# Layer 1 of a four-layer graph network: token transposes moved ahead of the softmax rows, layer-norm statistics moved behind both residual additions, bank order of queries and values swapped, and a copy moved ahead of the scatters at the layer's end

## The chip, the cores and the metric

The kernel runs on one core of a Trainium2 chip. The metric is the device time of one execution in microseconds (us). A core has five engines that run side by side, each with its own instruction stream: PE (matrix multiplications; its weight loads are listed as PEld), DVE (vector), ACT (activation functions and copies), POOL (a further vector engine, which here also issues the scatters) and SP (which issues most DMA transfers). [...]

## What is computed

The input `x` has 128 graphs of 64 nodes with 256 features, that is 8192 tokens; `adj` is a 64x64 adjacency shared by all graphs. Four layers follow each other, each of the form "layer norm of x plus f(x)":

```python
x = _layernorm(x + _L0_gnn_ref(x, adj, ...))   # dense attention over the 64 nodes
x = _layernorm(x + _L1_gnn_ref(x, ...))        # attention over 512 listed edges, 4 heads
x = _layernorm(x + _L2_gnn_ref(x, adj, ...))   # adj product, two matmuls, two batch norms
x = _layernorm(x + _L3_gnn_ref(x, adj, ...))   # two adj products, four LSTMs over windows
```

The change is in layer 1:

```python
Xq = (H @ W_lin.T).reshape(bt, n, h, dh)
Xv = (H @ W_val.T).reshape(bt, n, h, dh)
e = einsum('behd,hd->beh', leaky_relu(Xq[:, src] + Xq[:, dst], 0.2), a)
e = e + log(A0[src, dst] + EPS)
m = segment_max(e, src);  ex = exp(e - m[src]);  attn = ex / segment_sum(ex, src)[src]
Y = segment_sum(attn[..., None] * Xv[:, dst], src)
return Y.reshape(bt, n, d) @ W_out.T
```

## The kernel before

**Tiles.** The tokens are cut into 16 tiles `q` of 512 tokens (eight graphs each). Layers 0 and 1 run as one software pipeline over the 16 tiles: in step `q` the kernel does the edge work of tile `q` for layer 1, layer 0 for tiles `q + 1` and `q + 2`, the projections of layer 1 for tile `q + 1`, and the last steps of layer 1 for tiles `q - 3` and `q - 4`. Edge softmax is done for two tiles at once, a pair `S`; so a step with even `q` (from 2 on) also carries the softmax of the pair that has just been finished. Below, such a step is called a *pair step*, the other one a *plain step*.

**The steps.** `l0_e` ends layer 0 of a tile: residual, statistics and layer norm. `l1_t` transposes the 512 normalised tokens on PE (`transposed`, L227: two groups of four 128x128 transposes, each group into one bank, each copied out by ACT, L228). `l1_qv(q, c2)` projects half a tile: for each of two 128-token chunks it makes the queries (bank `pq`, L318) and the values (one bank `pv` for both chunks, L321); ACT and DVE take the queries out in turn (L328, L329, L330) and ACT copies the values (L331). `l1_graph` makes the edge sums `z` (L355), ACT takes the relu (L357); `reduce_heads` sums them with L346. `l1_softmax` and `l1_sums` do the scans on DVE (L367 to L374, then the exponential on ACT, L375, then L380 and L381, the last of which writes `dn`). `l1_weights` transposes the two softmax rows `e` and `dn` (L389, a bank each), takes a reciprocal on DVE (L395), multiplies (L397), scatters the result to DRAM with four indirect DMAs that POOL issues (L401), and SP loads it back as `ld` (L407). `v_a` has POOL copy `ld` into `am` (L414), multiplies on PE (L422, two banks) and copies with ACT (L426). `v_b` is the output projection (L436, two banks), the residual additions on DVE (L438), the statistics (L95, L96, L85, L98) and the layer norm on POOL (L86, then L100). `v_c` multiplies by the adjacency (L456). `l0_c` makes layer 0's scores: transposes L264, masks L267, L269, maximum L271, exponentials on ACT L274.

**Order.** A step lists what stands between its eight edge pieces. The list entries that matter here:

```python
[(l1_sums, S), (l0_b, q + 2)],
[(v_b, q - LAG - 1)],
[(l1_weights, S), (l1_t, q + 1), (l0_c, q + 2)],
[(sums, q), (l1_qv, q + 1, 0)],
[(v_c, q - LAG - 1), (v_a, q - LAG)],
```

A scheduler then places the instructions on each engine. `step` ties only PE's instructions to the list's order; DVE, ACT and POOL are ordered by the scheduler, from priorities and its own estimate of durations. So a change in the order of calls can also change the order on engines that it doesn't name. [...]

**Banks.** Layers 0 and 1 share three PSUM banks (5, 6 and 7 in the program) for everything called `m`: projections, transposes, `v_a`, `v_b`. A new use of a bank waits until its last reader is done. `z` has its own four banks, `e` one.

**The end of layer 1.** After step 15 the last pair's softmax and the last tiles' `v_a`, `v_b`, `v_c` remain. They are interleaved with blocks of layer 2's first matmul (`fill`; L749, eight matmuls of 512 columns each block, later the seven-product form L820). `given` keeps the order of the calls on PE, DVE, ACT and POOL, each call's instructions behind the last ones of the call before.

Of the kernel before, what the change touches and what calls it, by code (L numbers as in the profile page):

```python
# [8 lines left out]
F32 = mybir.dt.float32  # L9
# [8 lines left out]
P = 128  # L18
NB = 128
N = 64  # L20
D = 256
KD = D // P
HEADS = 4
# [3 lines left out]
NQ = 16  # L27
PQ = 4
# [13 lines left out]
def kernel(ctx: ExitStack, tc: tile.TileContext, i, out):  # L42
    nc = tc.nc
# [39 lines left out]
    def rsqrt(dst, var, n):  # L83

        nc.vector.tensor_scalar_add(dst, var, LN_EPS)  # L85
        nc.gpsimd.tensor_tensor(dst, dst, mhalf[:, :n], OP.pow)  # L86

    def layernorm(dst, src, n, engine):

        st = small.tile([P, n, 6], F32, name="ln_st", bufs=5)  # L90
        mv = small.tile([P, n, 2], F32, name="ln_mv", bufs=5)
        both = small.tile([P, 2, n], F32, name="ln_rs", bufs=5)
        rs, ng = both[:, 0, :], both[:, 1, :]
        for r in range(n):
            nc.vector.bn_stats(st[:, r, :], src[:, r, :])  # L95
            nc.vector.bn_aggr(mv[:, r, :], st[:, r, :])  # L96
        rsqrt(rs, mv[:, :, 1], n)
        nc.vector.tensor_scalar_mul(ng, mv[:, :, 0], -1.0)  # L98
        for r in range(n):
            engine.tensor_scalar(dst[:, r, :], src[:, r, :], ng[:, r:r + 1], rs[:, r:r + 1],  # L100
                                 op0=OP.add, op1=OP.mult)
# [8 lines left out]
    def given(do, *args, **more):  # L110
        traced = nc.cur_bb.bb.instructions
        first = len(traced)
        with ExitStack() as order:
            for e in latest.values():
                order.enter_context(tc.issue_after(e))
            r = do(*args, **more)  # L116
        for t in traced[first:]:
            if t.engine in (mybir.EngineType.PE, mybir.EngineType.DVE, mybir.EngineType.Activation,
                            mybir.EngineType.Pool):
                latest[t.engine] = t  # L120
        return r
# [8 lines left out]
    with ExitStack() as two:  # L130
# [7 lines left out]
        vp = values.enter_context(tc.tile_pool(name="vp", bufs=1, side="right"))  # L138
# [5 lines left out]
        def bank(shape, name="m", bufs=3):  # L144
            return (psm if name == "m" else ps).tile([P] + shape, F32, name=name, bufs=bufs)
# [85 lines left out]
        def token_major(q):  # L231

            return Aq(q).rearrange("p (c d) -> p c d", c=PQ)
# [70 lines left out]
        L1 = {}  # L304
# [5 lines left out]
        def l1_qv(q, c2):  # L310
            xT, v = L1[q]["xT"], L1[q]["v"]

            sp = spads[q // BPS % 2].rearrange("p (s e x b d h) -> p s e x b d h", e=2, s=2, x=2, b=BPS, d=2)
            pv = bank([2, D])
            for c in (2 * c2, 2 * c2 + 1):
                pq = bank([D + HEADS])
                for k in range(KD):
                    nc.tensor.matmul(pq, xT[:, k, c * P:(c + 1) * P], wq[:, k, :],  # L318
                                     start=k == 0, stop=k == KD - 1)
                for k in range(KD):  # L320
                    nc.tensor.matmul(pv[:, c % 2, :], xT[:, k, c * P:(c + 1) * P], wv[:, k, :],  # L321
                                     start=k == 0, stop=k == KD - 1)

                qs = work.tile([P, 2, D], F32R, name="qs", bufs=6)
                L1[q]["qs"].append(qs)
                for s in range(2):
                    r, ro = slice(s * N, (s + 1) * N), slice((1 - s) * N, (2 - s) * N)
                    nc.scalar.activation(qs[r, s, :], pq[r, :D], AF.Copy)  # L328
                    nc.vector.tensor_sub(qs[ro, s, :], pq[r, :D], qs[r, s, :].bitcast(F32))  # L329
                    nc.scalar.activation(sp[r, s, c % 2, 0, q % BPS, c // 2, :], pq[r, D:], AF.Copy, scale=SLOPE)  # L330
            nc.scalar.activation(v[:, 2 * c2:2 * c2 + 2, :], pv, AF.Copy)  # L331
# [75 lines left out]
                nc.sync.dma_start(ld[S][s * N:(s + 1) * N], half)  # L407


        def v_a(q):  # L410
            S, b = divmod(q, BPS)
            v = L1[q]["v"]
            am = vp.tile([P, PQ * HEADS, N], F32, name="am")
            nc.gpsimd.tensor_copy(am.rearrange("p (e r) n -> p e r n", e=2),  # L414
                                  ld[S].rearrange("p n (e b r) -> p b e r n", e=2, b=BPS)[:, b])
            pY = [bank([KD, PQ, N]) for _ in range(2)]
            for c in range(PQ):
                for h in range(HEADS):
                    for s in range(2):
                        r = slice(s * N, (s + 1) * N)  # L420
                        r0 = (h % 2) * 64
                        nc.tensor.matmul(pY[s][r0:r0 + 64, h // 2, c, :], v[r, c, h * 64:(h + 1) * 64],  # L422
                                         am[r, (c % 2) * 2 * HEADS + c // 2 * HEADS + h, :], start=True, stop=True)
            yT = L1[q]["yT"] = vp.tile([P, KD, PQ, 2, N], F32, name="yT")
            for s in range(2):
                nc.scalar.activation(yT[:, :, :, s, :], pY[s], AF.Copy)  # L426

        def v_b(q):
            yT = L1[q]["yT"]
            x1 = token_major(q)  # L430
            y = vp.tile([P, PQ, D], F32, name="y")
            for c2 in range(2):
                p_ = bank([2, D])
                for c in range(2):
                    for k in range(KD):
                        nc.tensor.matmul(p_[:, c, :], yT[:, k, 2 * c2 + c].rearrange("p s n -> p (s n)"),  # L436
                                         wout[:, k, :], start=k == 0, stop=k == KD - 1)
                nc.vector.tensor_add(y[:, 2 * c2:2 * c2 + 2, :], p_, x1[:, 2 * c2:2 * c2 + 2, :])  # L438
            x2 = L1[q]["x2"] = y
            layernorm(x2, y, PQ, nc.gpsimd)  # L440
            nc.sync.dma_start(x2_dram[q], x2.rearrange("p c d -> p (c d)"))

        def v_c(q, one=True):
# [125 lines left out]
        l0_d(1)  # L569
        l1_t(0)  # L570
        l1_qv(0, 0)
        l1_qv(0, 1)


# [86 lines left out]
        LAG = BPS + 1  # L661
# [4 lines left out]
        def step(do, n, *more):  # L666
            if not 0 <= n < NQ:
                return
            traced = nc.cur_bb.bb.instructions
            first = len(traced)  # L670
            if queue:
                with tc.issue_after(queue[-1]):
                    do(n, *more)
            else:
                do(n, *more)
            mine = [t for t in traced[first:] if t.engine == mybir.EngineType.PE]
            queue.extend(mine[-1:])
# [4 lines left out]
        for q in range(NQ):  # L682
            S = q // BPS - 1 if q % BPS == 0 else -1
            between = [
                [(l0_e, q + 1), (l0_a, q + 2)],
                [(sums, q if q else -1), (l1_softmax, S)],
                [(l1_sums, S), (l0_b, q + 2)],
                [(v_b, q - LAG - 1)],
                [(l1_weights, S), (l1_t, q + 1), (l0_c, q + 2)],
                [(sums, q), (l1_qv, q + 1, 0)],  # L690
                [(v_c, q - LAG - 1), (v_a, q - LAG)],
                [(l0_d, q + 2), (l1_qv, q + 1, 1)],
            ]
            for b in range(GQ):
                step(l1_graph, q, b)
                for do, n, *more in between[b]:
                    step(do, n, *more)
                if setup:
                    setup.pop(0)()
        sums(q)  # L700
        S = NQ // BPS - 1
# [55 lines left out]
        def up_block(q):  # L757
            for m in range(2):
                put(q, m, up(q, m))
                if m == 0:  # L760
                    last_tail()
            pz = [up(q, m) for m in (2, 3)]
            for m in (2, 3):
                put(q, m, pz[m - 2])
# [167 lines left out]
        def one(q):  # L932
            return lambda: up_block(q)

        def pair(q, g):
            return lambda: up_job(q, g, T[q])

        fill = [one(n) for n in range(7)] + [pair(n, g) for n in (7, 9) for g in range(2)]
        given(v_b, NQ - LAG - 1)
        fill.pop(0)()  # L940
        given(l1_sums, S)
        fill.pop(0)()
        given(v_c, NQ - LAG - 1, False)
        given(l1_weights, S)
        sums_at = {3: 7, 5: 9}
        for n, (do, q) in enumerate([(do, q) for q in range(NQ - LAG, NQ) for do in (v_a, v_b, v_c)]):
            given(do, q, *[False] * (do == v_c))
            fill[n]()
            if n in sums_at:
                T[sums_at[n]] = tile_sums(inputs(sums_at[n]))  # L950
        q = NQ - LAST - 1
# [1023 lines left out]
```

## Time and profile before

| | before |
|---|---|
| median of three timed runs | 2052.08 us (2048.62, 2052.08, 2052.64) |
| the profiled execution | 2051.53 us, of which the recorded span is 2049.7 us |
| mean granted clock of PE over the span | 0.986 of full speed |
| a pair step and a plain step together, in the middle of layers 0 and 1 | 61.25 us (the scan L372 starts at 231.12, 292.38, 353.63 us) |
| PE busy in 292 to 353 us | 58.06 of 61.00 us |
| layers 0 and 1 run until about | 523 us, their end beside layer 2 until about 616 us |

The span counts from the first to the last instruction; 1.83 us of the profiled execution lie around it. "Busy" counts an instruction from start to end; matmuls overlap, and their ends are modelled. In the answers quoted below, a line of the timeline gives start and length in us, engine, source line, operation, what it writes and reads, how many instructions are merged, and in brackets how long the engine stood idle before it and what released it. A line of the waits gives the total in us, how often, and the longest.

### The profile page before, as it was taken

To read this page: it belongs to the slowest core of one execution; us is meant where nothing else is said; L and a number is where in the kernel's file an instruction comes from. 1 tells how busy PE (TensorE), PEld (TensorE's weight loads), DVE (VectorE), ACT (ScalarE), POOL (GpSimd) and SP (SyncE) were. 2 spreads that over 40 slices of the span, in tenths; PEclk is the share of its full clock that TensorE was granted. 3 is DMA by queue.
4 is the path that set the end of the run, shared out by engine and by line. 5 is a ranking of instruction groups with operands and counts; after the bars stand their busy time and mean duration, and the time that the engine had idled before them with its cause. 6 is when DMAs were issued, how large, how long until landed. Compare 5 with 4: busy or idle time off the path is not lost.

```text
span 2049.7 us, 31505 instructions
## 1 busy us (share of the span) xinstructions
PE 1943.6 (95%) x11447; PEld 1332.9 (65%) x11447; DVE 1256.3 (61%) x2763; ACT 987.6 (48%) x1892; POOL 883.8 (43%) x1017
## 2 busy tenths in 40 slices
PE   5999999999899989899999999999999999999997
PEld 4666667766454435477677477677577667578685
DVE  7456665564457454765566865556775557764566
ACT  2766667666335633634343644343544333544333
POOL 1123334343345543564545543435443445444264
PEclk8999999999999999999999999999999999999998
DMA  5344443332112125432242243132143032131022
GB/s 134 79 65 68 79 69 54 66 50 39 37 29 60 41 103 171 158 136 98 112 143 85 77 140 139 42 126 91 52 153 120 21 113 65 44 119 78 0 65 70
DMA packets 236539, 173.84 MB, mean 85 GB/s; under 512 B 150624, under 2 KB 213600, under 8 KB 233056
## 3 DMA queue, kind: packets, MB, share of 16 engines
q1 hardware_dynamic: 234528, 169.86, 29.1%
q8 instruction: 90, 1.47, 0.3%
q0 software_dynamic: 1024, 1.05, 0.2%
q10 hardware_dynamic: 832, 0.92, 0.1%
q14 instruction: 65, 0.53, 0.1%
HBM read 110.18 MB, written 61.60 MB: 84 GB/s over the span
## 4 chain that ended last, share of the span: by engine, by line
PE 68%; DVE 17%; ACT 5%; POOL 4%; issue 4%; DMA 1%; SPq 0%; DVEq 0%; POOLq 0%; ACTq 0%
PE l L1700 25%; PE l L1656 7%; PE l L1437 4%; PE pz L820 4%; PE e L346 3%; PE m L318 2%; PE pz L749 2%; PE g L1336 2%; PE m L253 2%; PE m L321 2%; PE z L355 2%; PE pz L1017 2%; PE g L1324 2%; DVE ln_st L95 1%; DVE cell L1614 1%
## 5 line engine op out<-in xcount | busy, mean ns | idle before, releaser
L1700 PE MATMUL l<-xs,wx 128*128 128x256 f32 (+1 forms) x896 | 277.0, 400 | 5.7 <-DVE gate L1719 4.2
L1700 PE MATMUL l<-hs,wh 128*128 128x256 f32 (+1 forms) x896 | 276.5, 399 | 2.9 <-DVE hs L1564 2.1
L1715 ACT ACTIVATE kept<-l 128x256 f32<-128x256 f32 (+1 forms) x224 | 88.6, 402 | 332.2 <-PE l L1700 330.7
L86 POOL TENSOR_TENSOR ln_rs<-ln_rs,mhalf 128x2 f32<-128x2 f32 (+2 forms) x98 | 86.4, 882 | 338.1 <-DVE ln_rs L98 334.9
L1700 PE MATMUL l<-H,wx 128*128 128x256 f32 (+1 forms) x672 | 210.5, 402 | 4.3 <-DVE gate L1728 3.4
L1700 PE MATMUL l<-hid,wh 128*128 128x256 f32 (+1 forms) x672 | 208.8, 399 | 0.0
L1700 PEld LDWEIGHTS l<-xs,wx 128*128 128x128 f32 x896 | 168.6, 190 | 50.7 <-issue 5.8
L1700 PEld LDWEIGHTS l<-hs,wh 128*128 128x128 f32 x896 | 169.2, 190 | 46.8 <-DVE hs L1564 4.7
L1733 ACT ACTIVATE gate<-gate,bias 128x512 f32<-128x512 f32 (+1 forms) x280 | 170.6, 657 | 42.0 <-DVE gate L1724 34.8
L1656 PE MATMUL l<-H,wx 128*128 128x256 f32 (+5 forms) x672 | 185.2, 431 | 4.9 <-DVE H L116 2.7
L1656 PEld LDWEIGHTS l<-H,wx 128*128 128x128 f32 x672 | 118.8, 190 | 65.5 <-issue 34.2
L357 ACT ACTIVATE u<-z 128x1024 f32<-128x1024 f32 x128 | 130.3, 1025 | 63.4 <-PE z L355 62.6
L1700 PEld LDWEIGHTS l<-H,wx 128*128 128x128 f32 x672 | 125.7, 190 | 42.6 <-DVE gate L1728 7.4
L1700 PEld LDWEIGHTS l<-hid,wh 128*128 128x128 f32 x672 | 127.2, 190 | 32.0 <-issue 2.6
L1723 POOL TENSOR_TENSOR gate<-gate,kept 128x256 f32<-128x256 f32 (+1 forms) x84 | 64.9, 773 | 154.2 <-DVE kept L1721 153.9
L329 DVE TENSOR_TENSOR qs<-m,qs 64x256 fp32r<-64x256 f32 x128 | 54.1, 422 | 109.1 <-ACT qs L328 107.0
L355 PE MATMUL z<-gath_r,qs 128*128 128x512 f32 x256 | 99.9, 478 | 0.6 <-ACT u L357 0.4
L1622 ACT ACTIVATE gate<-cell 128x512 f32<-128x512 f32 (+1 forms) x88 | 58.6, 666 | 86.5 <-DVE cell L1614 64.5
L1568 POOL TENSOR_TENSOR hs<-hid 128x256 f32<-128x256 f32 (+1 forms) x28 | 27.4, 977 | 168.3 <-DVE hid L1600 85.2
L1728 DVE TENSOR_TENSOR gate<-l,gate 128x256 f32<-128x256 f32 (+1 forms) x112 | 50.0, 446 | 61.4 <-POOL gate L1723 36.4
L1610 POOL TENSOR_TENSOR cell<-gate,cell 128x512 f32<-128x512 f32 (+1 forms) x56 | 75.4, 1367 | 28.4 <-ACT gate L1733 28.4
L1717 DVE TENSOR_TENSOR gate<-l,kept 128x256 f32<-128x256 f32 (+1 forms) x112 | 49.2, 439 | 57.1 <-ACT gate L1733 32.9
(375 smaller groups left out, 4095.3 us busy)
## 6 DMA issues: line engine op xcount, KB each, us to landing
wx<-sums SPq DMA_DIRECT2D x9, 2048.0 KB
wh<-sums SPq DMA_DIRECT2D x9, 1792.0 KB
way<-st SPq DMA_DIRECT2D x54, 256.0 KB
st<-way SPq DMA_DIRECT2D x216, 64.0 KB
xin<-in_x SPq DMA_DIRECT2D x16, 512.0 KB
ld<-table SPq DMA_DIRECT2D x16, 512.0 KB
x_dram<-y SPq DMA_DIRECT2D x16, 512.0 KB
x2r<-x_dram SPq DMA_DIRECT2D x32, 256.0 KB
```

What stands on the lines that cost most here:

```text
L86: nc.gpsimd.tensor_tensor(dst, dst, mhalf[:, :n], OP.pow)
L346: nc.tensor.matmul(pes[S][n * CG:(n + 1) * CG, :], apad[:, k, CG - HEADS - r0:2 * CG - HEADS - r0], u[:, k, :], start=r0 == 0 and k == 0, ...
L355: nc.tensor.matmul(z[:, k, :], L1[q]["qs"][c][:, s, k * P:(k + 1) * P], gath_r, start=True, stop=True)
L357: nc.scalar.activation(u, z, AF.Relu)
L820: nc.tensor.matmul(self.bank[at], lhs, rhs, start=first and n == 0, stop=n == len(self.terms) - 1, skip_group_check=True)
L1437: nc.tensor.matmul(self.bank[at], lhs, rhs, start=new, stop=True, skip_group_check=True)
L1610: nc.gpsimd.tensor_tensor(c, t, c, OP.mult)
L1656: nc.tensor.matmul(b, w.raw[0][:, k, at, m, :], x, start=k == 0, stop=k == KD - 1)
L1700: nc.tensor.matmul(self.banks[j], lhs, rhs, start=src == 0, stop=src == 1)
L1715: nc.scalar.activation(self.keep(j), b, AF.Copy)
L1723: e.tensor_tensor(t[0][:, 1], t[0][:, 1], k[5], OP.add)
L1733: given(lambda: nc.scalar.activation(dst, dst, f, bias=b))
```

## The change

Five edits, in `l1_qv`, `v_a`, `v_b`, the step list and the code after the last step:

```diff
-            pv = bank([2, D])
+            pv = None
             for c in (2 * c2, 2 * c2 + 1):
                 pq = bank([D + HEADS])
+                if pv is None:
+                    pv = bank([2, D])
...
-        def v_a(q):
+        def v_m(q):
             S, b = divmod(q, BPS)
-            v = L1[q]["v"]
-            am = vp.tile([P, PQ * HEADS, N], F32, name="am")
+            am = L1[q]["am"] = vp.tile([P, PQ * HEADS, N], F32, name="am")
             nc.gpsimd.tensor_copy(am.rearrange("p (e r) n -> p e r n", e=2),
                                   ld[S].rearrange("p n (e b r) -> p b e r n", e=2, b=BPS)[:, b])
+
+        def v_a(q):
+            if "am" not in L1[q]:
+                v_m(q)
+            v, am = L1[q]["v"], L1[q]["am"]
...
-            layernorm(x2, y, PQ, nc.gpsimd)
+            with tc.issue_after(nc.cur_bb.bb.instructions[-1]):
+                layernorm(x2, y, PQ, nc.gpsimd)
...
-                [(l1_weights, S), (l1_t, q + 1), (l0_c, q + 2)],
+                [(l1_t, q + 1), (l1_weights, S), (l0_c, q + 2)],
...
+        given(l1_sums, S)
         given(v_b, NQ - LAG - 1)
         fill.pop(0)()
-        given(l1_sums, S)
+        given(v_m, NQ - LAG)
+        given(l1_weights, S)
         fill.pop(0)()
         given(v_c, NQ - LAG - 1, False)
-        given(l1_weights, S)
```

In words: the bank of the first queries is asked for before the bank of the values. The statistics of `v_b` may not be placed before its second residual addition. In each step the token transposes come before the softmax rows' transposes. At the end of layer 1, the last pair's sums come before `v_b` of tile 12, and the last pair's row transposes and scatters come one block of layer 2 earlier, with the copy `am` of tile 13 ahead of them on POOL.

The order that results on each engine, seen in the two built programs (no times are in it): the numbers of instructions and their operands are the same. On PE, in every pair step, the eight transposes L227 stand before the eight of L389, and the rest of layer 1 is in the same order; at the end, `L436, L749 x8, L389 x8, L749 x8, L456, L422` replaces `L436, L749 x16, L456, L389 x4, L749 x1, L389 x4, L749 x14, L422`. On DVE, both L438 stand before the eight statistics; in pair steps the reciprocal L395 follows behind all statistics of `v_b` (before, it stood ahead of the last of them), and the four L329 of the next projection come between L267, L269, L271 and L277. On ACT, in pair steps, the four exponentials L274 stand behind three of the four L328 (before, behind one), and the copy of the values L331 stands behind L274 and two more short instructions; in plain steps L274 stands behind one L328 (before, ahead of all). On POOL, in pair steps, the layer norm of `v_b` stands before all four scatters (before, the first scatter stood ahead of it). Waits for banks also change hands: the second row's transposes (L389, `dn`) take the bank that the first group of token transposes used, so they wait for ACT's L228 of that group; L318 of the first projection takes the bank of the `dn` row and waits for L395.

## The prediction

> **What bounds the kernel now.** I read the page's busy times and its chain first, then PE's waits over the middle of layers 0 and 1, then the timelines of one pair step, last the stretches in which PE's clock fell.
>
> ```profile
> span 2049.7 us, 31505 instructions
> PE 1943.6 (95%) x11447; PEld 1332.9 (65%) x11447; DVE 1256.3 (61%) x2763; ACT 987.6 (48%) x1892; POOL 883.8 (43%) x1017
> ...
> PE 68%; DVE 17%; ACT 5%; POOL 4%; issue 4%; DMA 1%; SPq 0%; DVEq 0%; POOLq 0%; ACTq 0%
> ```
>
> PE is the bound; no instruction goes, so only PE's idle time can. PE's waits from 170 to 540 us:
>
> ```profile
> PE m L318 <- ACT yT L426: 5.4, 10, 0.6
> PE m L227 <- ACT tT L228: 4.1, 6, 0.7
> PE m L227 <- issue: 3.3, 5, 0.7
> PE m L264 <- DVE ln_mv L96: 2.4, 5, 0.5
> PE m L389 <- DVE dn L381: 2.2, 1, 2.2
> ```
>
> Lines 2 to 5 all sit where rows and tokens are transposed in a pair step. The timeline of PE in one of them, and in the last one (q = 14):
>
> ```profile
> 301.48 0.64 PE L227 MATMUL m<-ident,A 128*128 128x128 f32 x4 [0.66 <-issue]
> 302.81 0.66 PE L227 MATMUL m<-ident,A 128*128 128x128 f32 x4 [0.69 <-ACT tT L228]
> 303.95 0.66 PE L264 MATMUL m<-ident,sb 128*128 128x128 f32 x4 [0.48 <-DVE ln_mv L96]
> 304.36 0.72 PE L355 MATMUL z<-gath_r,qs 128*128 128x512 f32 x2
> ...
> 314.89 1.15 PE L318 MATMUL m<-wq,tT 128*128 128x260 f32 x4 [0.56 <-ACT yT L426]
> ```
> ```profile
> 483.21 0.63 PE L389 MATMUL m<-ident,dn 128*128 128x128 f32 x4 [2.25 <-DVE dn L381]
> ...
> 490.78 1.15 PE L318 MATMUL m<-wq,tT 128*128 128x260 f32 x4
> ```
>
> The first wait is for the second addition (300.72 to 301.38), which stands behind half the statistics; the second for the one bank both token groups share; the third ends with the reciprocal (302.17 to 303.90), not with the L96 named. The other engines at the same place:
>
> ```profile
> 308.32 0.39 ACT L274 ACTIVATE e<-e,mx 128x128 f32<-128x128 f32 x1
> ...
> 310.71 0.58 ACT L331 ACTIVATE v<-m 128x512 f32<-128x512 f32 x1
> ```
>
> L422 needs that copy (done 311.29) and starts at 311.99: 0.7 us of slack. And the clock, by stretches:
>
> ```profile
> 122.40:129.00 6.60, 5.91 (x25) 2.92 (x28) 5.00 (x11) 2.89 (x6) 1.66 (x2) 0.50 0.76 98
> 484.00:490.60 6.60, 5.91 (x26) 2.07 (x24) 3.52 (x13) 2.22 (x3) 3.36 (x5) 0.50 0.02 5
> 554.90:557.50 2.60, 0.10 (x2) 0.01 (x2) 0.69 (x1) 0.69 (x1) 2.53 (x2) 1.00 0.05 13
> ```
>
> The seventh column is the granted clock: half speed for 6.6 us after the gaps at q = 2 (2.07 us) and q = 14 (2.25 us), at 5.91 us busy some 2.9 us lost each time; none after the gap of 2.50 us at 555, where L422 waits for POOL's copy behind four scatters.
>
> [...] L331 at 310.71 stands behind L274, and a late maximum delays the values. [...] L100 takes 4.24 us for four beside the scans (292.65), 2.16 otherwise (306.78).
>
> **The change part by part.** All from the timeline of 299 to 315 us, durations as they stand there; gains against the same instruction before.
>
> *Pair step, transposes.* PE is free at 299.79. L227's first group has its bank (copied at 297.1) and runs to 300.23; the second takes the bank of addition one (done 299.80) until 300.67; L389 of `e` that of addition two, now about 299.74 to 300.40: no wait. L389 of `dn` needs the first L228, which stands behind ACT's L357 (next instruction at 300.91), so 301.51 with its 0.60; start 301.56. L264 follows at 302.04, z at 302.45 instead of 304.36: gain 1.9.
>
> *Pair step, given back.* DVE now does all statistics first: 1.94 from 300.34 to 302.28 (as 289.51 to 291.45). Reciprocal to 303.94, one L267, four L397 (0.2 each), three L267: 305.84. L329 waits for ACT's L328, 1.18 behind L318's start (306.86, 308.04 before), now 304.95, so until 306.54; then L329, L269, L329, L271 at about 0.45 and 0.7: maximum at 308.8, before 307.4. ACT: L274 308.8 to 310.35, L330, L328, then L331 to 311.5. PE would start L422 at 304.95 + 5.13 = 310.08 and stands 1.45 for the values. ACT's next L357 starts at 311.51 (before: 312.08), L426 behind it, and L318, which waits for L426's bank, comes 0.57 earlier (314.32), no more. I take +0.57; bounds 1.9 (values not late) and -1 (maximum 1.5 later than worked out).
>
> *Plain step.* Addition two waits for PE (331.41) either way; two L95 and two L96 move behind it: the maximum comes 0.6 later (335.86 to 336.45). L274 now stands behind one L328 and ends at 338.5 instead of 337.45, but two L328 that stood behind it go with or ahead of it; L357 at 340.79 instead of 340.58, L318 0.2 later. Five pairs (q = 4 to 13): 5 x (0.57 - 0.21) = gain 1.8.
>
> *q = 2.* L227 fills the gap ahead of `dn`, its fourth row block waiting for L100 until 119.14. But `dn`'s bank waits for L228, behind two L357 (119.95 to 121.87): L389 at 122.43, 0.8 later than before (121.61). Behind the waiting L389 stand L264, z and L346, for which the layer-0 scores and ACT's relu wait; all move together. Then L264 122.92, z 123.3 instead of 125.33: gain 2.0. The gap is still 1.88, so the clock may fall again; at full clock the late maximum takes back what the clock gives, thus 2.0 either way; bounds 0.8 and 3.
>
> *q = 14.* No L95 stands between the scans: `dn` at 482.86 instead of 483.07. L389 at 482.9, z at 483.35 instead of 486.08, after a gap of 1.15: no fall of the clock. L318 waits for the reciprocal (484.97 to 486.7) and starts at 486.73 instead of 490.78: gain 4.05, of which 2.9 is the clock's. L100 now comes ahead of the scatters and is done at 490.4, L456 at 490.9.
>
> *q = 15.* Here PE waits on `v_b`'s chain: L438 (509.36), statistics, L86, L100, L414, L422 at 516.57, L426, L346 at 519.84. After the second addition stand four L95 instead of two: 1.78 to L85 instead of 1.1, loss 0.66.
>
> *The end.* Sums first: both scans at 528.2 to 530.8, additions and statistics behind, L98 at 534.5 instead of 530.6; L86 and L100 with 3.45 end at 539.1, the copy for tile 13 (1.9) at 541.0. PE: L436 to 526.1, a block of 6.95, L389 0.9, a block: L456 at 540.9, L422 at 541.95. No wait, 0.95 spare; the 2.50 go. Scatters from 541 at 2.9 each end at 550, SP's L407 starts about 553 (557.47 before), so tile 14's copy is no later. L456 of tile 13 waited 0.80 and stood stretched by 0.97 (2.07 against 1.1) for L100: L436 now stands 4 us further from it. Gain 4.3; the last tile's statistics again hold POOL, loss 0.3.
>
> *Scatters and SP.* In pair steps POOL now runs L86 and L100 first (302.3 to 305.6), then four scatters without the layer norm between them: at the 3.5 between the later ones before (309.12, 312.63, 316.19), from 305.7 to about 316.3, as late as before. So SP's L407 (318.33), the loads of x queued behind it, and the copy L414 (328.71, which ended on L407's landing) stand still: nothing. If POOL's spacing grew, L414 has 9 us until L422 at 340.52 needs it.
>
> *Bank order of queries and values.* L318 now waits for the reciprocal (303.94 against its own 304.95), so a reciprocal 1 us later would stop PE; L321 waits for L397 as before. In plain steps the first queries get the bank that is free first, as before. Nothing, with half a us either way for each pair of steps in the range.
>
> Sum: 2.0 + 1.8 + 4.05 - 0.66 + 4.3 - 0.3 = 11.2 us. After 616 us nothing differs, and PE's later waits are on DVE, ACT and POOL, so it carries to the end. The profiled execution's 2051.53 (span 2049.7, 1.83 around it) becomes 2040.3; the median lies 0.55 above that execution: **2041**.
>
> **The rivals.** *R1, everything is given back in the steps, and the clock's part is luck:* the values' wait takes the whole gain of a pair step (5 x -0.2 = -1.0), and an execution that keeps its clock gains only 0.8 at q = 2 and 1.15 at q = 14. 0.8 + 1.15 - 0.66 - 1.0 + 4.3 - 0.3 = 4.3 less than 2052.08: 2047.8. For it: three timings spread by 4 us, about the clock's price; against: the median is the higher kind. *R2, the values are not late:* if DVE runs ahead of my reckoning by 1.4, pair steps gain up to 1.9: 5 x 1.3 = 6.5 more, 2034.5. Against: the order on DVE puts L329 ahead of the maximum. *R3, slower:* the gap before L422 in each pair step grows from 1.45 to 2.1 us, a length at which the clock was seen to fall (2.07). It decides once L331 ends at 312.2, that is a maximum 0.7 later. Each of five steps then loses 0.65 and the clock's 2.9: 5 x 3.55 = 17.7 on top of 2041, about 2058.7; with the clock falling in every second one, 2051. For it: DVE's order in pair steps is the tightest of all. Against: a gap of 1.41 at 516 left the clock alone. *R4, POOL's copy is late at the end* (scans or L100 slower by 2): 2 us back, 2043, inside the range.
>
> **How the numbers follow.** A measurement tells about 0.2% here, 4.1 us. Forecast with R4 0.60, R1 0.18, R2 0.12, R3 0.10. Faster: forecast and R2 whole, R1 by a third (2048.0 is the border and R1 stands at 2047.8 with its own spread): 0.78; R1's rest and the mild form of R3 within 0.2%: 0.14; slower: R3 otherwise, 0.08. Range 2034.5 to 2048.5: R2, the forecast's own 2037 to 2045, R1.
>
> **What would show it.** In a pair step: no wait at L227, 0.3 to 0.5 at the second L389, 1.4 at L422 ending on L331, L318 about 0.6 earlier; the pair of steps at 60.9 us. No half clock near q = 14, L318 there 4 us sooner; no wait at L422 behind the scatters. Wrong if the period stays at 61.25 or grows, or if new half-clock stretches appear between 180 and 480 us.

## The result, and the profile after

The changed kernel takes 2044.78 us (median of nine runs, 2044.55 to 2046.24), the kernel before on the same chip 2050.94 (nine runs, 2048.32 to 2052.64): ratio 0.9971, 95% interval 0.9962 to 0.9980. It is 4 to 8 us faster, about half of the 11.2 us forecast, and inside the range. The profiled execution took 2044.78 us, its span is 2043.0.

The page of the changed kernel, first its busy times, then the shares of its chain:

```profile
span 2043.0 us, 31508 instructions
...
PE 1938.6 (95%) x11447; PEld 1335.4 (65%) x11447; DVE 1252.3 (61%) x2763; ACT 987.1 (48%) x1892; POOL 878.0 (43%) x1017
...
PE 69%; DVE 15%; ACT 5%; POOL 4%; issue 3%; DMA 2%; SPq 1%; DVEq 0%; POOLq 0%; ACTq 0%
```

PE has the same 11447 matmuls and is still the bound; its busy time is 5.0 us less though no instruction went: the same matmuls took less time, and a stretch at half clock is one of the things that make them longer (sixteen of `L253` took 6.34 us under it before, 3.75 at full clock after). PE's waits of the changed kernel from 170 to 540 us (total, times, longest):

```profile
PE m L428 <- ACT v L333: 7.2, 5, 1.4
PE m L320 <- ACT yT L432: 4.7, 10, 0.6
PE m L391 <- DVE y L444: 2.2, 1, 2.2
PE m L428 <- POOL am L415: 1.7, 1, 1.7
PE m L391 <- ACT tT L228: 1.5, 5, 0.3
PE e L348 <- ACT u L359: 1.2, 1, 1.2
PE z L463 <- POOL y L100: 1.0, 1, 1.0
```

(L318, L331, L389, L422, L436, L438, L456 of before are now L320, L333, L391, L428, L442, L444, L463.) The waits at L227 and L264, 9.8 us in all, are gone, and 7.2 us stand in a new place: five times 1.44 for the copy of the values. The timelines of PE and of ACT in the pair step at 300 us show both ends of it:

```profile
297.10 1.04 PE L227 MATMUL m<-ident,A 128*128 128x128 f32 x8
297.97 0.60 PE L391 MATMUL m<-ident,e 128*128 128x128 f32 x4
298.87 0.66 PE L391 MATMUL m<-ident,dn 128*128 128x128 f32 x4 [0.29 <-ACT tT L228]
...
309.12 1.16 PE L428 MATMUL m<-am,v 64*64 64x64 f32 x62 [1.44 <-ACT v L333]
...
311.76 1.14 PE L320 MATMUL m<-wq,tT 128*128 128x260 f32 x4 [0.39 <-ACT yT L432]
```
```profile
306.21 0.40 ACT L274 ACTIVATE e<-e,mx 128x128 f32<-128x128 f32 x1 [0.45 <-DVE mx L271]
...
308.46 0.60 ACT L333 ACTIVATE v<-m 128x512 f32<-128x512 f32 x1
```

ACT waits for DVE's maximum, runs the four exponentials, and only then copies the values for which PE stands. Two PE starts, of `v_c` in step after step, give the length of a pair step and a plain one together: 60.84 us (306.41 to 367.25), before 61.25 (311.00 to 372.25).

Where the time of the two profiled executions differs, stage by stage (start of the same PE instruction, after against before):

| stage | forecast gain | gain between the two profiles |
|---|---|---|
| up to 60 us, no changed instruction in it | 0 | 3.1 |
| q = 2 | 2.0 | 1.8 |
| q = 3 | 0 | -3.0 |
| q = 4 to 13 | 1.8 | 2.05 |
| q = 14 | 4.05 | 2.3 |
| q = 15 | -0.66 | -4.6 |
| the end of layer 1 | 4.3 - 0.3 | 3.7 |
| after 616 us | 0 | 1.4 |

The first and the last line are no work of the change. In the first 60 us `L253` took 6.34 us before and 3.75 after at the same place, because half clock covered it in one execution only; after 616 us PE's waits are the same within half a us each, but for one that is 1.0 us longer after, and half clock covers the last 12.6 us before and the last 9.8 after. So the changed stages gain 2.25 us between these two executions, and 4.5 us lie where the change has no part. The stages hold half clock too, 13.7 us of it before and 17.1 after between 60 and 640 us. What the change is worth on the average is therefore read from the timed runs, not from this pair.

### The profile page after: what moved, and what is told of

The parts are those of the page before. It is cut to its first block, busy times and chain, and to the rows that moved or that the text cites. A ratio compares the mean times of both kernels' runs of the same rounds, so it can differ in the third digit from the quotient of the medians.

```text
span 2043.0 us, 31508 instructions
## 1 busy us (share of the span) xinstructions
PE 1938.6 (95%) x11447; PEld 1335.4 (65%) x11447; DVE 1252.3 (61%) x2763; ACT 987.1 (48%) x1892; POOL 878.0 (43%) x1017
## 4 chain that ended last, share of the span: by engine, by line
PE 69%; DVE 15%; ACT 5%; POOL 4%; issue 3%; DMA 2%; SPq 1%; DVEq 0%; POOLq 0%; ACTq 0%
PE l L1708 25%; PE l L1664 7%; PE l L1445 4%; PE pz L827 4%; PE pz L756 3%; PE m L253 2%; PE e L348 2%; PE m L320 2%; PE m L442 2%; PE g L1344 2%; PE pz L1025 2%; PE z L357 2%; PE m L323 2%; DVE cell L1622 1%; PE g L1332 1%
## 5 line engine op out<-in xcount | busy, mean ns | idle before, releaser
L331 DVE TENSOR_TENSOR qs<-m,qs 64x256 fp32r<-64x256 f32 x128 | 53.9, 422 | 105.0 <-ACT qs L330 103.2
```

## The experiments

The kernels of one group below were timed on one chip beside the kernel before; its median there was 2050.1 (first group), 2052.7 (second), 2053.1 (third) and 2050.9 us (the last kernel). So ratios, not times, are compared between groups.

**One part alone.** Each edit was put into the kernel before; the fourth kernel is the changed one with the values' bank again asked for first.

```diff
swap_only:  [(l1_weights, S), (l1_t, q + 1), ..] -> [(l1_t, q + 1), (l1_weights, S), ..]
stats_only: + with tc.issue_after(nc.cur_bb.bb.instructions[-1]): layernorm(x2, y, ..)
end_only:   the edits of v_a, v_m and of the code after the last step
no_bank:    the changed kernel with  pv = bank([2, D])  ahead of the loop over c
```

> The kernel before, with the step list's swap alone (token transposes ahead of the softmax rows). Theory of the prediction: the swap is what takes the transposes' wait away, but with half the statistics still between the two additions the second group of L227 waits as before for addition two, so a pair of steps gets 0.2 to 0.6 us shorter (61.25 to about 60.85), q = 2 some 2 us shorter, nothing at the end: 1 to 4 us in all, about 2048. Rival, the parts need one another: the pair of steps stays at 61.25 and the time within 1 us of 2050.9. Rival, clock luck: no change in any period, only the first 60 us differ from run to run.

> The kernel before, with the statistics behind both residual additions alone. Theory of the prediction: in a plain step it costs 0.2, in a pair step it brings the rows' transposes forward by the 0.66 that the second addition waited but makes the layer-0 maximum and with it the values' copy later; q = 15 loses about 0.7. Pair of steps 60.9 to 61.4, total within 2 us of 2050.9, more likely above. Rival: it alone carries the gain of the steps (pair of steps at 60.85 or less, total 2047 or less).

> The kernel before, with the edits at the end alone (sums first, POOL's copy and the rows ahead of the scatters' wait). Theory of the prediction: 4.3 us from the wait of 2.5 at L422 and from q = 16, nothing anywhere else: 2046.6, with the pair of steps at 61.25 and the half-clock stretches near q = 2 and 14 still there. Rival: the end's gain is taken up later (PE's waits after 616 us grow), total 2050 or more.

> The changed kernel with the values' bank again taken first. Theory of the prediction: the order of the banks is worth nothing, 2044.8 within 1 us, pair of steps 60.84, the wait of some 1.4 for the values' copy still there. Rival: taking the queries' bank first is what made the wait at q = 3 grow to 2.3 or the values late; then without it the losses at q = 3 and q = 15 (3.0 and 4.6 us) go and the time is 2038 to 2041. Second rival: it carries a part of the steps' gain, then the pair of steps is above 61.

| kernel | ratio to before, 95% interval | pair and plain step |
|---|---|---|
| swap_only | 0.9997 (0.9989 to 1.0005) | 61.08 |
| stats_only | 1.0007 (0.9999 to 1.0015) | 60.98 to 61.44, on average 61.16 |
| end_only | 0.9979 (0.9969 to 0.9989) | 61.25 |
| no_bank | 0.9966 (0.9954 to 0.9979) | 60.84 |

The end alone brings 0.21%, 4.3 us, as forecast. Neither step edit brings anything alone. In the trace of swap_only, the timeline of PE shows in a pair step the wait of 0.64 that was expected there, now at the rows `e`, and at q = 15 a wait for POOL's copy that was not:

```profile
301.59 1.04 PE L227 MATMUL m<-ident,A 128*128 128x128 f32 x8
303.26 0.66 PE L389 MATMUL m<-ident,e 128*128 128x128 f32 x4 [0.64 <-DVE y L438]
...
517.80 1.98 PE L422 MATMUL m<-am,v 64*64 64x64 f32 x64 [4.96 <-POOL am L414]
```

There POOL starts the first scatter of q = 14 at 491.53, behind the layer norm of `v_b` (before: 487.10, ahead of it), and the second starts 5.56 later, so the rows come back from DRAM only at 515.8. In this profile that wait alone, 4.96 against 1.41 before, takes back some 3.5 us of what the swap gives in the other steps. In stats_only, PE's timeline of a pair step shows the waits of before moved on by one group:

```profile
302.06 0.66 PE L227 MATMUL m<-ident,A 128*128 128x128 f32 x4 [0.69 <-ACT tT L228]
303.40 0.66 PE L264 MATMUL m<-ident,sb 128*128 128x128 f32 x4 [0.69 <-ACT tT L228]
...
314.86 1.14 PE L318 MATMUL m<-wq,tT 128*128 128x260 f32 x4 [1.06 <-ACT yT L426]
```

What the additions give at the transposes is taken back at `L318`, 1.06 instead of 0.56. The bank order is worth nothing that can be told: no_bank keeps the period of 60.84 and the wait of 1.44, and the intervals of the two ratios overlap. Its rival, that the bank order made the losses at q = 3 and q = 15, is out too: the wait at q = 3 is still 2.07, and the clock still falls at q = 15.

**The steps' edits together, and the odd tiles.** Second group, with the two kernels of the next two paragraphs.

```diff
steps_only: the changed kernel without the edits at the end
stats_even: with tc.issue_after(..) only  if q % BPS == 0
```

> The changed kernel without the edits at the end: swap, statistics and bank order only. Theory that the parts add up: the swap alone (ratio 0.9997) and the statistics alone (1.0007) make nothing together, 2050.9. Theory that the two need one another (the swap only pays when the second addition no longer stands behind half the statistics): 2 to 3 us faster than before, 2047.5 to 2048.5, pair of steps at 60.84 against 61.08 (swap alone) and 61.16 (statistics alone), and the wait for the values' copy of 1.4 back in each pair step.

> The changed kernel with the statistics behind both additions only in even tiles, which the pair steps and the end's first tile take; the plain steps and q = 15 (tile 11) are as before. Theory: in q = 15 the layer norm of tile 11 is 0.66 earlier, so the two waits there (0.99 for L100's rows, 1.67 for POOL's copy) shrink by about 0.66 together, and the clock falls there less often; plain steps within 0.1 each. 0.7 to 3 us better than the changed kernel: 2042 to 2044. Rival, the odd tiles do not matter and what was lost at q = 15 was the grid of the clock's windows alone: waits of 2.6 stay, time within 1 us of 2044.8.

steps_only: ratio 0.9987 (0.9979 to 0.9995), 2.7 us; pairs of steps from 60.85 to 61.06. Alone the two step edits come to +0.04% together, in one kernel to -0.13%. The difference, 0.17% with some 0.14 of uncertainty from three intervals, and the periods (0.17 and 0.09 us gained alone, 0.33 together, on average) both point to swap and statistics needing one another, but neither by much; swap_only's loss at q = 15 is a part of it. 2.7 and end_only's 4.3 make 7.0; the changed kernel measured 5.9 (0.29% of 2050.9; 4.1 to 7.8), so the parts add up within their error.

stats_even: ratio 0.9961 (0.9947 to 0.9975). PE's timeline at q = 15, stats_even first and then the changed kernel:

```profile
507.74 2.08 PE L465 MATMUL z<-aht,y 64*64 64x64 f32 x64 [0.34 <-POOL y L100]
511.24 1.99 PE L428 MATMUL m<-am,v 64*64 64x64 f32 x64 [1.42 <-POOL am L415]
```
```profile
507.56 2.07 PE L463 MATMUL z<-aht,y 64*64 64x64 f32 x64 [0.99 <-POOL y L100]
511.30 1.99 PE L428 MATMUL m<-am,v 64*64 64x64 f32 x64 [1.67 <-POOL am L415]
515.61 3.64 PE L348 MATMUL e<-u,apad 128*32 128x512 f32 x16 [1.17 <-ACT u L359]
```

The wait for the layer norm falls by 0.65, where the later statistics had been priced at 0.66; with 0.25 at POOL's copy the way from `v_b` to `v_a` falls from 11.79 to 10.90 us (before: 10.87). But the half clock behind it stays (510.74 to 520.98), so this was not what cost most at q = 15.

**What halves the clock.** The edges of the half-clock stretches, worked out from the granted clock in slices of 0.2 us, lie within 0.01 us on a grid of 3.413 us, in the traces of before, of after and of all experiments; only its offset against the start of the span differs from execution to execution (2.72 us before, 2.23 after). With the grid known, each of its windows can be asked for PE's busy time. The stretches of the changed kernel (window, length, busy us of PE, PEld, DVE, ACT, POOL, clock, DMA):

```profile
152.42:155.83 3.41, 1.65 (x66) 1.57 (x67) 1.00 (x3) 3.24 (x9) 0.22 (x1) 1.00 0.03 5
155.83:159.24 3.41, 3.41 (x12) 2.77 (x11) 0.00 (x0) 2.53 (x5) 1.77 (x1) 0.50 0.00 0
476.68:480.10 3.42, 1.17 (x9) 0.96 (x10) 3.38 (x5) 1.64 (x3) 0.00 (x0) 1.00 0.00 0
480.10:483.51 3.41, 3.41 (x17) 1.71 (x18) 3.17 (x12) 1.02 (x1) 0.00 (x0) 0.50 0.00 0
507.40:510.82 3.42, 1.84 (x64) 1.29 (x64) 0.00 (x0) 1.26 (x2) 3.20 (x5) 1.00 0.50 120
510.82:521.06 10.24, 8.59 (x85) 3.74 (x86) 0.00 (x0) 2.11 (x3) 2.01 (x4) 0.50 0.05 18
```

Each half-clock stretch follows a full-clock window in which PE was busy for 1.84 us or less of 3.41. At the first of these places no_bank has a wait of 2.07 instead of 2.31 and its grid 0.2 us further on; its stretches there:

```profile
152.62:156.03 3.41, 1.85 (x67) 1.68 (x68) 0.85 (x2) 3.25 (x9) 0.41 (x1) 1.00 0.02 5
156.03:159.44 3.41, 3.41 (x19) 2.92 (x18) 0.56 (x2) 2.89 (x8) 1.60 (x1) 1.00 0.00 0
```

No fall. And in stats_even one of two pair steps with the same wait of 1.44 fell:

```profile
244.50:247.91 3.41, 1.69 (x65) 1.40 (x64) 0.60 (x2) 3.30 (x8) 0.96 (x1) 1.00 0.30 52
247.91:251.33 3.42, 3.42 (x11) 2.73 (x11) 0.00 (x0) 2.59 (x5) 0.96 (x1) 0.50 0.05 14
```

Over the 14 traces of before, after and the experiments, the full-clock windows from 60 to 640 us divide like this:

| PE busy in the window (of 3.41 us) | windows | followed by half clock |
|---|---|---|
| up to 1.50 | 18 | 17 |
| 1.51 to 1.94 | 37 | 16 |
| 1.95 to 2.09 | 38 | 2 |
| 2.10 and more | 2219 | 0 |

So in these traces whether the clock falls goes with PE's work in the window: with up to 1.50 us it fell in 17 windows of 18, with 2.10 or more in none of 2219, between them sometimes. The length of a gap alone does not tell: before's gap of 2.50 us at 555, longer than the two behind which it fell (2.07 and 2.25), was divided between two windows, and the emptier one kept 1.60 us of work, where it goes either way. To try idle time as the cause, work was added to the kernel before that nothing needs:

```diff
+for n in range(4 * EC if row is e and S in (0, NQ // BPS - 2) else 0):
+    nc.tensor.transpose(p_[:, n % EC, :], row[:, n % EC * P:(n % EC + 1) * P], ident)
```

> The kernel before, with the transposes of the rows e done five times instead of once in the two steps q = 2 and q = 14 (16 more TensorE instructions each, same result in the same bank, some 1.7 us of PE in the gap of 2.07 and 2.25 ahead of the second rows' transposes). Theory of the clock: PE's share of the window no longer falls below what keeps the clock, no half-speed stretch near 122 and 484 us, and about 2 x 2.9 us less, 2044.5 to 2046. Rival, the half clock comes from something else or the extra work counts as load and brings it on: stretches stay, 2050.1 or up to 2 us above.

Ratio 0.9978 (0.9968 to 0.9989): 32 TensorE instructions more, and some 4.5 us faster. The timeline of PE of before_warm at q = 14:

```profile
478.15 1.91 PE L391 MATMUL m<-ident,e 128*128 128x128 f32 x16
480.57 0.63 PE L389 MATMUL m<-ident,dn 128*128 128x128 f32 x4 [0.51 <-DVE dn L381]
```

The rows `dn` still wait for their scan at the end; the gap is only filled, and neither place falls. In before, end_only and stats_only, which have both gaps, both places fell. So here the idle time ahead of them brought the half clock on: six falls at six places with the gap left open, none at two with it filled. As the filling shortens the gap too (2.25 to 0.51 us), this run does not tell length and share of a window apart. In this trace the clock fell at 511.90 and 556.27 instead; its eight runs spread from 2044.26 us (mean clock 0.990) to 2051.4 (0.987). The spread goes with the clock, as three thousandths of 2045 us are 6.1; that the 4 us between the three timings of before have the same cause is likely, but no trace of each was taken.

**The values' copy.** The exponentials of layer 0 are put behind it in pair steps.

```diff
+if q % BPS == 0 and q > BPS:
+    late.enter_context(tc.issue_after(L1[q - 1]["copied"]))
 for c in range(PQ):
     nc.scalar.activation(e[:, c, :], e[:, c, :], AF.Exp, ..)
```

> The changed kernel with ACT's four exponentials of layer 0 put behind the values' copy in pair steps, nothing else. Theory (the copy is late because it stands behind the exponentials, which wait for the maximum): the wait of 1.4 at the values' 64x64 matmuls goes to 0.3 or less in all five pair steps and the 2.3 at q = 3 to below 1; but the copy of yT then stands behind the exponentials, so the queries of the second half wait 1.0 to 1.4 for it instead of 0.4: pair of steps 60.84 to about 60.4, 2 to 3 us in all, 2042. Rival (the copy waits for PE or DVE, not for its place): wait of 1.4 stays, nothing changes. Second rival: everything is given back at yT, pair of steps 60.8, 2044.8.

Ratio 0.9958 (0.9944 to 0.9971), its interval over that of the changed kernel. The copy does move, and the wait at `v_a` goes, but PE then waits at the relation matmul for ACT's `u`, 0.66 to 1.79 us in each of the five pair steps; the timelines of ACT and of PE of this kernel in the same pair step (its L340, L281, L436, L365, L440 are the values' copy, the exponentials, `v_a`, the relation matmul and the copy of yT):

```profile
306.08 0.60 ACT L340 ACTIVATE v<-m 128x512 f32<-128x512 f32 x1 [0.29 <-PE m L330]
...
307.27 0.40 ACT L281 ACTIVATE e<-e,mx 128x128 f32<-128x128 f32 x1
```
```profile
308.24 1.13 PE L436 MATMUL m<-am,v 64*64 64x64 f32 x63
310.32 0.73 PE L365 MATMUL z<-gath_r,qs 128*128 128x512 f32 x2 [0.95 <-ACT u L367]
...
311.72 1.14 PE L327 MATMUL m<-wq,tT 128*128 128x260 f32 x4 [0.24 <-ACT yT L440]
```

`v_a` starts 0.9 us sooner, and the second half's queries at 311.72 instead of 311.76, as the second rival said: they end up behind the same maximum, exponentials and copies on ACT. A pair of steps takes 60.78 us, 0.06 less, and once 62.31, where the clock fell behind the wait of 1.79. So the place of the copy in ACT's order is not the bound of the pair step. The timelines point to the time of the maximum on DVE and to ACT's work from there to yT: in the changed kernel the maximum L271 (305.49) stands on DVE behind two of the query copies L331, the first of which waits 0.83 us for ACT. No run moved the maximum, so this is read from the timelines and not shown.

**Towards a better version.** tail moves `v_c(11)` and `v_a(12)` of q = 15 behind the last softmax matmul, so that PE has work during the chain of layer norm and copy. after_warm repeats transposes in the gaps of the changed kernel at q = 2 (rows `e`) and q = 14 (second token group). all_best is both and exp_late; all_best2 also puts the first block of layer 2 ahead of `v_b(12)`.

```diff
-                [(v_c, q - LAG - 1), (v_a, q - LAG)],
+                [(v_c, q - LAG - 1), (v_a, q - LAG)] if q < NQ - 1 else [],
...
         given(l1_softmax, S)
+        given(v_c, NQ - LAG - 2)
+        given(v_a, NQ - LAG - 1)
```

> The changed kernel with v_c(11) and v_a(12) of q = 15 put behind the last scores and the last softmax matmul, so that PE has 4 more relation matmuls and two groups of score sums to run while tile 11's layer norm and POOL's copy for tile 12 are under way. Theory: what q = 15 lost (4.6 us against the kernel before) are the waits of 0.99 and 1.4 to 1.7 and the half clock that they and the two stretched 64x64 groups bring; then both waits are 0.3 or less, no half clock near 510, and the time is 2.5 to 4.5 us below the changed kernel: ratio to before 0.995 to 0.996. Rival: the chain of layer norm, copy, yT and v_b only moves its wait to v_b(12) or to the rows of the last softmax; ratio 0.997 as the changed kernel.

> The changed kernel with work repeated in its two long gaps: the rows e transposed five times at q = 2, the second token group transposed five times at q = 14 (16 more TensorE instructions each, same values into the same bank). Theory of the window's activity: no half clock at 480 in any execution and none at q = 2; the changed kernel pays 1.5 to 3 us at 480 in most executions, so 1 to 3 us less: ratio 0.9955 to 0.9965. The wait of 2.2 at the rows e shrinks to about 0.5, that of 2.0 at the rows dn to about 0.3, and nothing starts later. Rival: the repeats delay the copies behind them and cost 1 us or more, ratio 0.998.

> The changed kernel with the three together: exponentials behind the values' copy in pair steps, v_c(11) and v_a(12) behind the last softmax matmul, and the repeated transposes at q = 2 and q = 14. If they add up: ratio to before 0.992 to 0.994, half clock only in the first 60 us. If the clock merely falls elsewhere instead: 0.996.

> The three together as in the run before it, and the first block of layer 2 ahead of v_b(12) instead of behind it. There v_b(12) waited 3.32 for the copy of yT, which stands on ACT behind the exponential of the last softmax. Theory: eight layer-2 matmuls (about 3.6 us more PE work) now stand in that gap, the wait is 0.3 or less, no half clock follows it near 515, and some 3 to 5 us go: ratio to before 0.991 to 0.993. Rival: the gain is taken back at the rows of the last softmax and the copy for tile 13, which come later by the block; ratio 0.9945.

| kernel | ratio to before, 95% interval | half clock, 60 to 640 us of its profile |
|---|---|---|
| changed kernel | 0.9971 (0.9962 to 0.9980) | 17.1 us |
| after_warm | 0.9955 (0.9942 to 0.9968) | 13.7 us |
| tail | 0.9934 (0.9921 to 0.9947) | 13.7 us |
| all_best | 0.9946 (0.9933 to 0.9959) | 10.2 us |
| all_best2 | 0.9948 (0.9935 to 0.9962) | 3.4 us |

The last column is one execution of each: tail's slowest (2046.14 us, of 2037.38 to 2046.14) and all_best2's fastest. In after_warm neither gap brings half clock any more, as expected; q = 15 still costs three windows. In tail the waits at q = 15 go, but the rival was right on where: a wait of 3.7 at `v_b(12)` for the copy of yT takes their place. The ratio is lower than the 0.995 to 0.996 expected all the same; no run shows why. all_best neither adds up (0.992 to 0.994) nor loses as much as feared (0.996); its trace shows where the wait comes from, first ACT's timeline, then PE's:

```profile
513.74 0.63 ACT L387 ACTIVATE e<-e 128x512 f32<-128x512 f32 x1 [7.72 <-DVE e L386]
514.28 1.01 ACT L479 ACTIVATE A<-z 128x1024 f32<-128x1024 f32 x1
515.18 1.08 ACT L444 ACTIVATE yT<-m 128x512 f32<-128x512 f32 x2
```
```profile
516.31 6.56 PE L454 MATMUL m<-wout,yT 128*128 128x256 f32 x16 [3.32 <-ACT yT L444]
```

The copy stands behind the exponential of the last softmax, and that behind three DVE operations. With a block of layer 2 in between (all_best2), `v_b(12)` runs without a wait, and no half clock follows, but the ratio is the 0.9945 of the rival and not the 0.991 to 0.993 of the theory:

```profile
515.95 3.70 PE L772 MATMUL pz<-A,w 128*128 128x512 f32 x8 [0.63 <-ACT A L479]
519.48 3.62 PE L454 MATMUL m<-wout,yT 128*128 128x256 f32 x16
```

Its profiled execution took 2037.5 us; its five runs, 2037.54 to 2041.97, lie below every run of the changed kernel. The runs of before on its chip have the same median as those beside the changed kernel (2050.92 and 2050.94), so this is a version that beats before by about 0.5%, and the changed kernel, which was not timed beside it, by about 0.2%: their intervals just meet. Tail's and all_best's ratios lie as low or lower, on another chip; the intervals of the three overlap, and which of them is best stays open.

## Why the prediction was right in sign, and half in size

By its own steps:

- *Pair step, transposes, and given back*: right. No wait at L227, 0.29 at the second L391, 1.44 at L428 on the values' copy (1.45 worked out), a gain of 0.45 for 0.57.
- *Plain step*: 0.04 lost instead of 0.21. Five pairs gain 2.05 for 1.8.
- *q = 2*: 1.8 for 2.0. The gap stayed (2.02), and the clock happened to hold.
- *q = 3*, not in the sum: -3.0. PE stood 2.31 at `v_a(0)` for the values' copy instead of 0.90, and the window fell. The copy was late because DVE's second mask L269, which stands ahead of the maximum, took 2.52 us instead of 0.69: it met POOL's copy `am`. POOL's and DVE's lines, the changed kernel first and then stats_even:

```profile
146.59 1.97 POOL L415 COPY am<-ld 128x1024 f32<-128x1024 f32 x1 [3.37 <-DMA ld<-table]
146.60 2.52 DVE L269 SCALAR_TENSOR_TENSOR e<-e 128x512 f32<-128x512 f32 x1
```
```profile
147.71 2.26 POOL L415 COPY am<-ld 128x1024 f32<-128x1024 f32 x1 [3.65 <-DMA ld<-table]
147.43 0.69 DVE L269 SCALAR_TENSOR_TENSOR e<-e 128x512 f32<-128x512 f32 x1
```

  In the four traces in which DVE starts first (stats_even) or the two do not overlap, L269 takes 0.69 and the wait at `v_a(0)` is 0.89 or 0.90; in the ten in which it starts within the copy it takes 1.01 to 2.52 and the wait is 0.90 to 2.31, the longer the earlier it starts. The prediction looked for no such meeting here. That they met is luck: in the changed kernel DVE came 0.01 us too late.
- *q = 14*, 4.05 claimed, 2.3 seen: the gap did not shrink to 1.15, it moved. With the token groups ahead, the rows `e` take the bank that the second addition reads, and here this addition stands on DVE behind the scan. DVE's and PE's timelines of the changed kernel:

```profile
477.74 1.22 DVE L383 TENSOR_TENSOR_SCAN dn<-seg,up 128x512 f32<-128x512 f32 x1
478.88 0.67 DVE L444 TENSOR_TENSOR y<-m,A 128x512 f32<-128x512 f32 x1
```
```profile
476.12 1.35 PE L227 MATMUL m<-ident,A 128*128 128x128 f32 x8
479.70 0.73 PE L391 MATMUL m<-ident,e 128*128 128x128 f32 x4 [2.24 <-DVE y L444]
```

  The step followed the wait for `dn` and took the bank of `e` as free, as it is in the other pair steps. The clock then fell for one window instead of two. That is about 1.4 of the 2.3, an estimate: half of PE's busy time at half clock, 6.14 us before and 3.41 after.
- *q = 15*, -0.66 claimed, -4.6 seen: the largest miss. The 0.66 of the statistics is there (0.65 in stats_even's difference), but it was priced as a wait alone. It comes on top of a wait for POOL's copy, and PE's window there has 1.84 us of work in it (before: 2.0 in the two windows there, and no fall). With half clock for three windows behind it, the way from the start of `v_a` to that of the next `v_b` (516.57 to 522.65 before, 511.30 to 521.04 after) takes 9.74 us instead of 6.08: 3.7 of the 4.6. In the one trace of each of the six kernels with the step edits and q = 15 in the old place, the clock fell there, as in swap_only and stats_only; with the old steps (before, end_only, before_warm) once in three.
- *The end*: 3.7 in the pair of profiles, 4.3 by end_only alone, for 4.0. No wait at L428 behind the scatters; L428 took 2.03 at 540.19 all the same.
- *Scatters and SP*, *bank order*: nothing, as costed, in the changed kernel; swap_only shows that the order on POOL at q = 14 can cost 5 us at q = 15 when the first scatter goes behind the layer norm. In the changed kernel the first scatter of q = 14 still stands ahead of it, at 483.68, unlike in the other pair steps.

Of the rivals, R1 was right that what the clock takes varies from execution to execution (the two profiles lie 3.1 us apart in the first 60 us, without a changed instruction there), and wrong that pair steps give everything back: 2047.8 was too slow. R2 fell with the 1.44 at L428. R3's mechanism exists, though in none of the changed kernel's pair steps: in six kernels (the changed one, no_bank, steps_only, stats_even, after_warm, tail) the clock fell in one of 18 pair steps with a gap of 1.44, and in two of 12 in which the matmuls of `v_c` took about 2 us instead of 1.16 and the gap was 0.62 to 0.71. Its threshold of 2.1 us for the gap was wrong in kind, since the falls go with the window's work. R4 did not come.

Three steps failed. At q = 14 the bank of the rows `e` was taken as free, and PE waited 2.24 us for it. At q = 3 the meeting of DVE and POOL was left out, 1.41 us and a window at half clock. At q = 15 it was assumed that a gap of 1.2 to 1.7 leaves the clock alone and one of 2.1 halves it, and the 3.7 us of half clock were priced at nothing; the reason given against R3, a gap of 1.41 at 516 that had left the clock alone, rested on this too. In this pair of profiles the three come to 8.7 us less than forecast.

Not tried: another order on DVE for the second addition at q = 14 or for the maximum in pair steps, holding back POOL's copy at q = 3, and a kernel whose offset to the grid is set on purpose.

## What to carry to other kernels

Here the half clock came and went only on a grid of 3.413 us, and from 60 to 640 us only behind windows with 2.09 us of PE work or less (35 of 93). Where traces show the like, price a gap by the PE work that is left in a window around it, add the half-speed windows behind it as a chance, and compare medians of many runs: a single pair of profiles differed here by 4.5 us in stretches without any change and by 2.25 us in the changed ones. A wait removed in front of a chain through several engines is given back at the next place where PE meets that chain; follow the chain to the operation that it ends in (here, as the timelines read, DVE's maximum, ACT's exponentials and copies) before counting the gain. Where an instruction takes longer beside one of another engine, as DVE's `L269` did here beside POOL's copy (up to 2.52 us instead of 0.69), ask at every place which of them comes first. When groups change places in an engine's order, follow every bank of the ring to its new releaser in every variant of the step, above all in those at the two ends of the loop.

## What was not expected of the hardware

- The grid: all half-clock edges of 14 traces lie at multiples of 3.413 us with one offset per execution. From 60 to 640 us windows with up to 1.50 us of PE work in 3.41 were followed by half clock in 17 of 18 cases, and with 1.51 to 1.94 in 16 of 37.
- The way back is sharper: over the same 14 traces and stretch, a half-clock window with 2.79 us of PE work or less was followed by another in 16 of 16 cases, one with 2.99 or more by full clock in 33 of 33.
- Busy time does not settle the cases between 1.51 and 1.94: 1.84 us at q = 15 fell in four of four windows, while 1.85 in no_bank at 152.62 and 1.89 in end_only at 511.10 held. All of them hold mostly 64x64 matmuls; the four that fell have one group of 64 in them that took 2.07 us, the two in which the clock held have 67 and 96 instructions. Whether such a slow group counts less than its time was not tried.
- A group of 64 matmuls of 64x64 takes 1.16 us or 2.0 to 2.08 at full clock, at the same places in most kernels (2.07 at 507.56 and 2.03 at 540.19 in the changed kernel, 1.16 at 513.55 in end_only). At 507.56 it starts in four parts of 16, at 507.56, 508.10, 508.64 and 509.17, each 0.05 to 0.06 us behind the end of one of the four instructions of L100. In six kernels (steps_only, stats_even, after_warm, exp_late, tail, all_best) `v_c` turned from the one to the other from the third pair step on. No run shows why, nor why it takes 2.03 at 540.19.
- DVE's L269 ended 0.55 to 0.56 us behind POOL's copy in all ten traces in which it started within it; so it took 1.01 to 2.52 us there, and 0.69 in the other four.
- Sixteen more transposes in each of two gaps, of 2.07 and 2.25 us, made a kernel 0.22% faster than leaving PE idle there.
